# The gate's 1x1 taken for four gates at once, with common mixing tiles, and the map sets' loads moved to ScalarE's queue

## The chip, the cores and the metric

The kernel runs on one core of a Trainium2 chip. The metric is the device time of one execution, in microseconds (us). Before the change it is 9507.76 us, the median of three runs (9506.13 to 9532.57).

## What is computed

There are eight batch elements of 8 channels x 512 x 512 in float32. Layer 0 normalises the channels in groups, multiplies a few of their lowest Fourier modes and adds the result back. Layer 1, cut to what matters here (x is the normalised input):

```
grid = x
for _ in range(15):
    mapped  = 3.9 * grid * (1 - grid)
    physics = 0.7 * mapped + 0.3 * conv3x3(mapped, K, one kernel per channel)
    grid    = 0.85 * physics + 0.15 * x
cml = clip(grid, 0.0001, 0.9999)
nca = sigmoid(conv1x1(relu(conv3x3(x, Wp)), Wu))            # 8 -> 128 -> 8 channels
g   = sigmoid(conv1x1(relu(conv3x3([x, cml, nca], Wg1)), Wg2))   # 24 -> 8 -> 8, the gate
out = g * cml + (1 - g) * nca                               # then the layer's residual is added
```

## The kernel before, in words

All of it is one program, whose order is written by a planner in Python: every engine executes its instructions in the order of the source. The unit of the plan is a tick, one call of `turn` (L1044) and in it of `work` (L1013). An element takes 67 or 68 ticks, and each tick mixes work of three kinds.

- **Map steps.** The 15 steps of the map run on sets: a `Slabs` object holds 16 slabs of 32 rows, and a set has one step in every second or third tick. A tick takes two steps. `convolve` (L518) issues 48 products in 32x32 tiles on TensorE: row of tiles h takes slab group h and writes PSUM bank `ps[h // 2][..., h % 2]`, column t writes 32 partitions of it. `settle` (L531) adds the drive on VectorE (L537), squares on ScalarE (L543) and renews the slabs' edge rows by transfers within SBUF (`renew`, m<-m, L570 and L571). A set's inputs are eight loads of 256 KB, dE and dO (L495), made ahead by `Phase.fetch` (L687); the squares of the first input are L502, the drives on GpSimd L516 and L547.
- **Hidden rounds.** Up to two rounds of the 8 -> 128 convolution (`Hidden.round`, L715: 24 matmuls each, L723, relu half on ScalarE L729 and half on VectorE L731), then the 128 -> 8 product of two rounds (`Hidden.point`, L738: L742, read out by a copy on ScalarE L749 or an addition on VectorE L751, sigmoid L755, stored by L758 one tick later). Their input is cols, 512 KB for four rounds (L706).
- **Others.** The layer 0 pieces of the element after this one (`spectral`), and the gates of the element before (`Gate`, L765).

A gate makes 12 rows. Its `load` brings gin, three transfers on SyncE's queue (L778: 384, 320 and 320 KB), and mix, the same rows of x, cml and nca, three transfers of 192 KB on 96 partitions (L783). `conv` computes the 3x3 in 12 matmuls (L793), blends x and nca on VectorE (L799), subtracts on GpSimd (L798) and applies the relu on VectorE (L803). A tick later `point` does the 1x1: three products of 128 x 32 (L810), each of two passes on the chip, then the sigmoid (L814) and a product on GpSimd (L816). In the next tick `finish` adds (L821) and stores 192 KB (L828). There are 43 gates an element, 344 in all.

`Others.feed` (L902) issues the gate's loads and the spectral pieces' loads of x early in the tick, before the second step's renewals; `transfers` then calls `Phase.fetch`. All these transfers are issued by SyncE. PSUM is four pairs of banks; `near` and `far` are two of them each and change roles, so that what a tick's gate and hidden point write is next written by the second step of the following tick. SBUF's big tiles come from 20 slots, which `sets` and `shared` divide by limits set tick by tick (`SHARED, MORE, LEAST`, L66).

After the last element 80 hidden rounds and all of its 43 gates are left; they run in ticks without map steps (L1090), two rounds and one gate each, here called the last stage.

Of the kernel before, what the change touches and what calls it, by code (L numbers as in the profile page):

```python
# [35 lines left out]
F32 = mybir.dt.float32  # L36
AF = mybir.ActivationFunctionType
ALU = mybir.AluOpType
# [79 lines left out]
def conv_layers(ctx: ExitStack, tc: tile.TileContext, a, out):  # L118
# [76 lines left out]
    gband = load("w_g1", [P, 3, 32])  # L195
    gpoint = load("w_g2", [P, GR * C])
    b_p = load("b_p", [HID, 1])
# [117 lines left out]
    def layer0(e, bank):  # L315
# [89 lines left out]
        def close(g, mv):  # L405

            mean, rstd, std = yield from group_stats(mv, 1, bank)
            nc.vector.tensor_copy(means[:, 0, g : g + 1], mean)
            nc.vector.tensor_copy(means[:, 1, g : g + 1], std)
            for c in (2 * g, 2 * g + 1):  # L410
                xt = e.x[C + c]
                nc.vector.tensor_scalar(xt, xt, mean, rstd, ALU.subtract, ALU.mult)

                def store(c=c, xt=xt):
                    nc.sync.dma_start(
                        out=e.xn[1 : N + 1, c].rearrange("(p j) w -> p j w", j=4), in_=xt
                    )
                    e.done_with(C + c)
                    e.closed.append(c)

                later(1, store)
# [48 lines left out]
    class Slabs:  # L470
# [14 lines left out]

        def load(self, o, h):
            if h == 0:
                self.d[o] = sets.take([P, 4, N], "dO" if o else "dE")
            if h == 3:
                self.loaded[o] = now[0]  # L490
            at, dims = self.source(o, h)
            to = self.d[o][32 * h : 32 * h + 32]
            if len(dims) == 4:
                to = to.rearrange("p (a b) w -> p a b w", a=2)
            nc.sync.dma_start(out=to, in_=view(self.e.xn, C * N + at, dims))  # L495

# [159 lines left out]
    class Phase:  # L656
# [7 lines left out]

        def load(self):
            s, o, h = self.loads.popleft()
            s.load(o, h)

# [18 lines left out]
        def fetch(self, n):  # L687
            while n - self.at >= -AHEAD and self.loads:
                s, _, h = self.loads[0]
                begun = sum(0 in x.d or x.m is not None for x in self.sets)  # L690
                if not h and sets.room() <= begun - self.squared or len(s.e.closed) < C:
                    break
                self.load()

# [70 lines left out]
    class Gate:  # L765


        def __init__(self, e, first):
            self.e, self.first, self.r0 = e, first, min(first, N - GR)

        def load(self):

            r0, self.at = self.r0, now[0]
            self.gin = shared.take([P, 4, N], "gin")
            self.mix = shared.take([P, 4, N], "mix")
            for q, src in enumerate((self.e.xn, self.e.cml, self.e.nca)):
                at, rows = (0, 48, 88)[q], (6, 5, 5)[q]
                nc.sync.dma_start(  # L778
                    out=self.gin[at : at + rows * C],
                    in_=view(src, r0 * C * N, [[N, rows * C], [3 * C * N, 4], [1, N]]),  # L780
                )
            for q, src in enumerate((self.e.xn, self.e.cml, self.e.nca)):
                nc.sync.dma_start(  # L783
                    out=self.mix[: GR * C, q],
                    in_=view(src, (r0 + 1) * C * N, [[N, GR * C], [1, N]]),
                )

        def conv(self, ps):

            gin, (x1, d, ng) = self.gin, (self.mix[: GR * C, q] for q in range(3))  # L790
            for n, (dx, lo, hi, at) in enumerate(SHIFTS):
                for j in range(4):
                    nc.tensor.matmul(  # L793
                        ps[32 * j : 32 * j + 32, lo:hi], gband[:, dx], gin[:, j, at : at + hi - lo],
                        start=(n == 0), stop=(n == 2), tile_position=(0, 32 * j),
                    )

            nc.gpsimd.tensor_tensor(d, d, ng, ALU.subtract)  # L798
            nc.vector.scalar_tensor_tensor(  # L799
                x1, x1, self.e.back[: GR * C, 1:2], ng, ALU.mult, ALU.add  # L800
            )
            shared.drop(gin)
            nc.vector.tensor_scalar(self.mix[:, 3], ps, b_g1, 0.0, ALU.add, ALU.max)  # L803

        def point(self, ps):
            mix = self.mix
            ps = ps[: GR * C]
            for j in range(3):
                at = slice(32 * j, 32 * j + 32)
                nc.tensor.matmul(  # L810
                    ps[at], gpoint[:, at], mix[:, 3], start=True, stop=True,
                    tile_position=(0, 32 * j),
                )
            nc.scalar.activation(mix[: GR * C, 2], ps, AF.Sigmoid, bias=b_g2[: GR * C])  # L814
            d = mix[: GR * C, 1]
            nc.gpsimd.tensor_tensor(d, d, mix[: GR * C, 2], ALU.mult)  # L816

        def finish(self):

            x1, o = (self.mix[: GR * C, q] for q in range(2))  # L820
            nc.vector.scalar_tensor_tensor(  # L821
                o, o, self.e.back[: GR * C, 0:1], x1, ALU.add, ALU.add
            )
            self.store()

        def store(self):
            lo = self.first - self.r0
            nc.sync.dma_start(  # L828
                out=view(
                    out, self.e.b * C * N * N + self.first * N,  # L830
                    [[N, GR - lo], [N * N, C], [1, N]],
                ),
                in_=self.mix[C * lo : GR * C, 1],
            )
            shared.drop(self.mix)

    class Element:


        def __init__(self, b):  # L840
# [11 lines left out]
            self.hidden = Hidden(self)  # L852
            self.gates = deque(Gate(self, r) for r in range(0, N, GR))
            self.back = sm.tile([P, 2], F32, name="back", bufs=3)
            self.x, self.at, self.fetched = {}, {}, 0
# [37 lines left out]
    class Others:  # L893


        def __init__(self):
            self.before, self.after, self.limit = None, None, 2
            self.mapped, self.paused = deque(), False
            self.loaded, self.convolved, self.pointed = deque(), deque(), deque()
            self.longs = 0  # L900

        def feed(self, t):  # L902
# [5 lines left out]
            kept = max(0, after.most() - len(after.x)) if spectral else 0  # L908
            while e and e.gates and t >= GATES_FROM and not self.paused:
                if len(self.loaded) == self.limit or shared.room() - kept < 2:  # L910
                    break
                if e.rows < min(e.gates[0].r0 + GR + 1, N) or len(e.mapped) <= 2 * SETS:
                    break
                g = e.gates.popleft()
                g.load()
                self.loaded.append(g)
            if spectral:
                after.fetch()

        def busy(self):  # L920
            return self.before.gates or self.loaded or self.convolved or self.pointed

        def finish(self):
            while self.pointed:
                self.pointed.popleft().finish()

        def point(self, ps):
            if not (self.convolved and self.convolved[0].at < now[0]):
                return False
            g = self.convolved.popleft()  # L930
            g.point(ps)
            self.pointed.append(g)
            return True

# [9 lines left out]
        def gate(self, ps):  # L944
# [4 lines left out]
            g.conv(ps)  # L949
            g.at = now[0]  # L950
            self.convolved.append(g)
            return True
# [40 lines left out]
    for n in count():  # L993
# [9 lines left out]
        while (  # L1003
            len(e.closed) >= C // 2 and len(first.loads) > 8 * (SETS - 2) and sets.room()
        ):
            first.load()
    tick(end=True)
# [4 lines left out]

    def work(steps, rounds, e, after, transfers, squares=lambda: None):  # L1013

# [12 lines left out]
        next(settled, None)  # L1027
        squares()

        if rounds == 2:  # L1030
            pairs.reverse()
        elif rounds:
            near, far = far, near
        point = rounds and e.hidden.n % 2 == 0
        gate = others.gate(near[0][:, 0])
        others.spectral((far[0], far[1]) if gate else (near[0], far[0] if point else near[1]))
        if point:
            e.hidden.point(near[1][:, 0])
        if not others.point(near[0][:, 1]):
            others.spectral([near[0] if gate or point else near[1]])  # L1040
        tick()
        squares()

    def turn(at, rounds, e, after, t):  # L1044
# [4 lines left out]
        def transfers():  # L1049
            others.feed(t)  # L1050
            for p in now_phases:
                p.fetch(at)

        def squares():
# [5 lines left out]
        steps = [slots[i] for i in (at, at + 1) if 0 <= i < len(slots)]  # L1060
        work(steps, rounds, e, after and after.hidden, transfers, squares)

# [86 lines left out]
```

## Time and profile before

| | |
|---|---|
| median of three runs | 9507.76 us |
| the profiled execution | 9539.07 us, span 9537.3 us |
| mean granted TensorE clock | 0.981 |
| TensorE matmul busy | 9076.3 us, 95% of the span |
| VectorE, ScalarE, GpSimd busy | 58%, 43%, 18% |
| transfers | 1326.71 MB, 53.5% of 16 engines' time on SyncE's queue |

The profile is one execution. PE is TensorE's matmuls, PEld its weight loads, DVE VectorE, ACT ScalarE, POOL GpSimd, SP SyncE; SPq is SyncE's queue of transfers. A group's line has the source line, the engine, the operation, the tiles (out<-in), the shape and count, then busy us and mean ns, and after the second bar the idle time before it and what ended most of it. "issue" is idle time for which no wait is seen. In the timeline a line has its start, its duration and how many instructions were merged. An element's ticks are counted from 0.

### The profile page before, as it was taken

To read this page: it belongs to the slowest core of one execution; us is meant where nothing else is said; L and a number is where in the kernel's file an instruction comes from. 1 tells how busy PE (TensorE), PEld (TensorE's weight loads), DVE (VectorE), ACT (ScalarE), POOL (GpSimd) and SP (SyncE) were. 2 spreads that over 40 slices of the span, in tenths; PEclk is the share of its full clock that TensorE was granted. 3 is DMA by queue.
4 is the path that set the end of the run, shared out by engine and by line. 5 is a ranking of instruction groups with operands and counts; after the bars stand their busy time and mean duration, and the time that the engine had idled before them with its cause. 6 is when DMAs were issued, how large, how long until landed. Compare 5 with 4: busy or idle time off the path is not lost. (4 is left out here: it accounts for less than half of the span.)

```text
span 9537.3 us, 330619 instructions
## 1 busy us (share of the span) xinstructions
PE 9076.3 (95%) x148976; PEld 4075.3 (43%) x148976; DVE 5572.4 (58%) x5820; ACT 4071.8 (43%) x4285; POOL 1671.2 (18%) x1286
## 2 busy tenths in 40 slices
PE   6999999999999999999999999999999999888999
PEld 3444444444444444444444444444444444333433
DVE  5665566655665556655566555665556655454555
ACT  2444444444444444444444444444434444333432
POOL 2010111112121121211212121021211212122122
PEclk9999999999999999999999999999999999999999
DMA  4241365565555555555555546555464555565288
GB/s 146 87 127 35 90 165 137 148 142 137 157 152 142 140 130 146 160 133 136 153 135 162 146 117 172 131 158 133 120 175 131 156 142 123 138 157 139 70 203 196
DMA packets 626870, 1326.71 MB, mean 139 GB/s; under 512 B 75258, under 2 KB 80762, under 8 KB 597970
## 3 DMA queue, kind: packets, MB, share of 16 engines
q1 hardware_dynamic: 623104, 1304.42, 53.5%
q8 instruction: 1170, 19.17, 0.9%
q14 instruction: 242, 1.98, 0.1%
q10 hardware_dynamic: 2354, 1.14, 0.0%
HBM read 977.48 MB, written 270.61 MB: 131 GB/s over the span
## 5 line engine op out<-in xcount | busy, mean ns | idle before, releaser
L524 PE MATMUL pair<-m,band 32*32 32x512 f32 x103680 | 3719.4, 607 | 208.7 <-issue 124.1
L543 ACT ACTIVATE m<-m 128x1024 f32<-128x1024 f32 x2016 | 2124.5, 1055 | 2438.6 <-DVE m L537 2293.2
L723 PE MATMUL pair<-cols,w_p 32*128 32x511 f32 (+1 forms) x24576 | 2860.0, 603 | 44.8 <-ACT y L749 14.4
L524 PEld LDWEIGHTS pair<-m,band 32*32 32x32 f32 x103680 | 2005.0, 103 | 1856.4 <-issue 1052.5
L537 DVE SCALAR_TENSOR_TENSOR m<-pair,dO 128x1024 f32<-128x1024 f32 x1152 | 1356.6, 1219 | 1218.4 <-PE pair L524 973.3
L723 PEld LDWEIGHTS pair<-cols,w_p 32*128 32x128 f32 x24576 | 1310.0, 186 | 1612.4 <-issue 1158.8
L537 DVE SCALAR_TENSOR_TENSOR m<-pair,dE 128x1024 f32<-128x1024 f32 x1008 | 1187.0, 1219 | 1142.4 <-PE pair L524 902.9
L731 DVE TENSOR_SCALAR h<-pair,b_p 128x1024 f32<-128x1024 f32 x1024 | 1313.0, 1283 | 877.8 <-PE pair L723 873.4
L729 ACT ACTIVATE h<-pair,b_p 128x1024 f32<-128x1024 f32 x1024 | 1140.6, 1114 | 902.5 <-PE pair L723 902.1
L816 POOL TENSOR_TENSOR mix<-mix 96x512 f32<-96x512 f32 x344 | 438.0, 1273 | 4302.2 <-ACT mix L814 4053.3
L742 PE MATMUL pair<-h,w_u 128*32 128x512 f32 x8192 | 1059.1, 610 | 47.6 <-ACT h L729 47.5
L793 PE MATMUL pair<-gin,w_g 128*32 128x511 f32 (+1 forms) x8256 | 964.7, 600 | 4.0 <-DMA gin<-nca 2.0
L798 POOL TENSOR_TENSOR mix<-mix 96x512 f32<-96x512 f32 x344 | 442.2, 1285 | 1423.4 <-DMA mix<-nca 1134.4
L547 POOL TENSOR_SCALAR dO<-dO 128x2048 f32<-128x2048 f32 x72 | 394.5, 5491 | 1009.4 <-DVE m L537 1009.1
L742 PEld LDWEIGHTS pair<-h,w_u 128*32 128x32 f32 x8192 | 244.1, 110 | 698.1 <-issue 329.2
L755 ACT ACTIVATE y<-y,b_u 128x512 f32<-128x512 f32 x256 | 184.8, 722 | 816.9 <-DVE y L751 816.9
L793 PEld LDWEIGHTS pair<-gin,w_g 128*32 128x32 f32 x8256 | 234.5, 110 | 684.6 <-issue 463.1
L749 ACT COPY y<-pair 128x512 f32<-128x512 f32 x256 | 150.1, 586 | 634.4 <-PE pair L742 487.2
L803 DVE TENSOR_SCALAR mix<-pair,b_g 128x512 f32<-128x512 f32 x344 | 258.2, 750 | 263.0 <-PE pair L793 262.5
L810 PE MATMUL pair<-mix,w_g 128*32 128x512 f32 x2064 | 370.7, 605 | 41.9 <-DVE mix L803 38.9
L821 DVE SCALAR_TENSOR_TENSOR mix<-mix,back 96x512 f32<-96x512 f32 x344 | 313.5, 911 | 144.2 <-POOL mix L816 144.2
L516 POOL TENSOR_SCALAR dO<-dO,base 128x512 f32<-128x512 f32 x288 | 208.4, 741 | 1075.6 <-DMA dO<-xn 923.9
(87 smaller groups left out, 2632.2 us busy)
## 6 DMA issues: line engine op xcount, KB each, us to landing
gin<-xn SPq DMA_DIRECT2D x344, 384.0 KB
cols<-xn SPq DMA_DIRECT2D x256, 512.0 KB
x<-in_x SPq DMA_DIRECT2D x120, 1024.0 KB
gin<-cml SPq DMA_DIRECT2D x344, 320.0 KB
gin<-nca SPq DMA_DIRECT2D x344, 320.0 KB
dE<-xn SPq DMA_DIRECT2D x288, 256.0 KB
dO<-xn SPq DMA_DIRECT2D x288, 256.0 KB
mix<-xn SPq DMA_DIRECT2D x344, 192.0 KB
```

The source lines that it names most:

```text
L524: nc.tensor.matmul(ps[h // 2][32 * t : 32 * t + 32, h % 2], band[at, self.channel(step - 1, h, t), dx], m[at, t, dx : dx + N], start=(n == ...
L537: nc.vector.scalar_tensor_tensor(u[:, at], ps[q], FLOOR, d[:, at], ALU.max, ALU.add)
L543: nc.scalar.square(u[:, at], u[:, at])
L547: nc.gpsimd.tensor_scalar(d, d, 0.5, None, ALU.add)
L723: nc.tensor.matmul(ps[g // 2][:, g % 2, lo:hi], w_p[p, dx, i % 2], self.cols[p, i // 2, at : at + hi - lo], start=(n == 0), stop=(n == 2), ...
L729: nc.scalar.activation(h[:, :2], ps[0], AF.Relu, bias=b_p)
L731: nc.vector.tensor_scalar(h[:, 2:], ps[1], b_p, 0.0, ALU.add, ALU.max)
L742: nc.tensor.matmul(ps[32 * g : 32 * g + 32], w_u[:, r % 4], h[:, g], start=(r == self.hs[0][0]), stop=(r == self.hs[-1][0]), tile_position ...
L793: nc.tensor.matmul(ps[32 * j : 32 * j + 32, lo:hi], gband[:, dx], gin[:, j, at : at + hi - lo], start=(n == 0), stop=(n == 2), tile_positi ...
L798: nc.gpsimd.tensor_tensor(d, d, ng, ALU.subtract)
L810: nc.tensor.matmul(ps[at], gpoint[:, at], mix[:, 3], start=True, stop=True, tile_position=(0, 32 * j),)
L816: nc.gpsimd.tensor_tensor(d, d, mix[: GR * C, 2], ALU.mult)
```

## The change

The old Gate keeps only gin and its 3x3; four gates make a Quad. Their relu results go to one tile (one gate in each of four columns, the partition quarters rotated by the gate's number k), and one 1x1 of 16 products of 32x32 serves all four. Four times three rows, with 24 lines used of 32, stand on the partitions, so gpoint is [128, 32] and the mixing tiles ng, d and x1 are 128 x 4 x 512 for a quad, each loaded by four transfers of 256 KB and stored by some twelve of 64 KB. The blend is done for a quad at once on GpSimd, in halves on VectorE, one tick or more after the last of the three tiles was asked for. `feed` moves to the end of the tick, behind both steps' renewals; loads of x stay where they were (`fetch`). The map sets' loads from tick 0 on (n >= 0) are issued by ScalarE, after the relus and squares of the tick.

```diff
-            nc.sync.dma_start(out=to, in_=view(self.e.xn, C * N + at, dims))
+            queue.dma_start(out=to, in_=view(self.e.xn, C * N + at, dims))
...
-                self.load()
+                self.load(nc.scalar if n >= 0 else nc.sync)
...
     class Gate:
         def conv(self, ps):
...
+                    to = 32 * ((j + self.k) % 4)
                     nc.tensor.matmul(
-                        ps[32 * j : 32 * j + 32, lo:hi], gband[:, dx], gin[:, j, at : at + hi - lo],
-                        start=(n == 0), stop=(n == 2), tile_position=(0, 32 * j),
+                        ps[to : to + 32, lo:hi], gband[:, dx], gin[:, j, at : at + hi - lo],
+                        start=(n == 0), stop=(n == 2), tile_position=(0, to),
                     )
...
+            nc.vector.tensor_scalar(quad.relu[:, self.k], ps, b_g1, 0.0, ALU.add, ALU.max)
...
+    class Quad:
+        def load(self):
+            src = (self.e.nca, self.e.cml, self.e.xn)[len(self.mix)]
+            t = shared.take([P, 4, N], ("ng", "d", "x1")[len(self.mix)])
+            for j in range(4):
+                nc.sync.dma_start(
+                    out=t[32 * j : 32 * j + 32, : self.n],
+                    in_=view(
+                        src, (self.r0 + 1 + 3 * j) * C * N,
+                        [[N, 32], [GR * C * N, self.n], [1, N]],
+                    ),
+                )
...
+        def blend(self):
+            n, (ng, d, x1) = self.n, self.mix
+            nc.gpsimd.tensor_tensor(d[:, :n], d[:, :n], ng[:, :n], ALU.subtract)
+            for k in (0, 2):
+                k1 = min(k + 2, n)
+                nc.vector.scalar_tensor_tensor(
+                    x1[:, k:k1], x1[:, k:k1], self.e.back[:, 1:2], ng[:, k:k1], ALU.mult, ALU.add
+                )
...
+        def point(self, near):
+            n, relu, (_, d, _) = self.n, self.relu, self.mix
+            for k in (1, 3, 0, 2):
+                for j in range(4 if k < n else 0):
+                    at, to = 32 * ((j + k) % 4), 32 * j
+                    nc.tensor.matmul(
+                        near[k // 2][to : to + 32, k % 2], gpoint[at : at + 32],
+                        relu[at : at + 32, k], start=True, stop=True, tile_position=(at, to),
+                    )
+            for k in (0, 2):
+                k1 = min(k + 2, n)
+                nc.scalar.activation(
+                    relu[:, k:k1], near[k // 2][:, : k1 - k], AF.Sigmoid, bias=b_g2
+                )
+                nc.gpsimd.tensor_tensor(d[:, k:k1], d[:, k:k1], relu[:, k:k1], ALU.mult)
...
     def work(steps, rounds, e, after, transfers, fetch, feed, squares):
...
         squares()
+        fetch()
...
+        others.blend()
+        quad = others.point()
         gate = others.gate(near[0][:, 0])
...
         if point:
             e.hidden.point(near[1][:, 0])
-        if not others.point(near[0][:, 1]):
+        if quad:
+            quad.point(near)
+        else:
             others.spectral([near[0] if gate or point else near[1]])
+        feed()
         tick()
```

`Others.feed` asks for one slot a gate where it asked for two, then for the mixing tiles of a quad whose gates have all been loaded, as many as there are slots for:

```diff
+            for quad in self.quads:
+                while not quad.gates and len(quad.mix) < 3 and shared.room() > kept:
+                    quad.load()
```

`Quad.finish` adds one half of the quad (a 128 x 2 x 512 instruction on VectorE) at each of its calls in a tick and stores after the second.

## The prediction

> **What bounds the kernel now.** I read the page's busy shares and groups first, then the chain of waits near its end, then the timeline of a few ticks, and last a table of stretches.
>
> ```profile
> PE 9076.3 (95%) x148976; PEld 4075.3 (43%) x148976; DVE 5572.4 (58%) x5820; ACT 4071.8 (43%) x4285; POOL 1671.2 (18%) x1286
> ...
> L810 PE MATMUL pair<-mix,w_g 128*32 128x512 f32 x2064 | 370.7, 605 | 41.9 <-DVE mix L803 38.9
> ```
>
> PE is the bound: 95%, against 58% on DVE. The group L810 is the 1x1 that changes: 344 gates of 6 matmul instructions. Its 605 ns are ends that overlap, so the price of a gate is read from the chain, where PE hands over from group to group:
>
> ```profile
> 9200.64 5.36 PE pair L723 x48
> 9205.99 2.71 PE pair L793 x24
> 9208.70 1.72 PE pair L742 x16
> 9210.42 0.85 PE pair L810 x6
> 9211.27 5.36 PE pair L723 x48
> ```
>
> A tick of the last stage is these four, 10.63 us with no gap, 0.85 us of it the 1x1. A tick in the middle, by the timeline, is this:
>
> ```profile
> 4501.22 6.58 PE L524 MATMUL pair<-m,band 32*32 32x512 f32 x192
> ...
> 4517.40 1.03 PE L810 MATMUL pair<-mix,w_g 128*32 128x512 f32 x6
> ...
> 4517.65 0.69 DVE L751 TENSOR_TENSOR y<-y,pair 128x512 f32<-128x512 f32 x1 [0.89 <-PE pair L742]
> ...
> 4518.36 6.58 PE L524 MATMUL pair<-m,band 32*32 32x512 f32 x192
> ```
>
> The tick is 17.14 us, again packed; its first block, 192 instructions in 32x32 tiles, ends at 4507.73: 12 waves of 16 in 6.51 us, 0.543 each. Where PE does stop, the transfers are behind it. These lines are from a tick in which the loads of two gates were issued together:
>
> ```profile
> 6418.69 0.44 SPq L778 DMA_DIRECT2D gin<-xn  x1
> ...
> 6434.21 1.91 PE L524 MATMUL pair<-m,band 32*32 32x512 f32 x3 [4.34 <-issue]
> ...
> 6439.23 1.26 POOL L798 TENSOR_TENSOR mix<-mix 96x512 f32<-96x512 f32 x1 [6.32 <-DMA mix<-nca]
> ```
>
> Twelve loads, 3.28 MB, took 20.5 us from the first issue to the end of the wait for the last, 160 GB/s, and meanwhile PE stood 4.3 us inside a block with no wait of its own. The last stage is closest to the limit of the transfers; four ticks, with the columns span, PE, PEld, DVE, ACT, POOL, clock, DMA share, GB/s:
>
> ```profile
> 9185.00:9227.50 42.50, 42.50 (x380) 15.23 (x376) 23.77 (x23) 14.02 (x17) 9.95 (x8) 1.00 0.86 213
> ```
>
> PE is busy 42.5 of 42.5 us, and the transfers already fill 86%.
>
> **The change, part by part.** Where ticks and orders of the changed program are named, they are from the listings of the two built programs.
>
> 1. *The old 1x1 goes.* 344 x 0.853 us (17.14 less 16.29, a tick without it: 6.51 + 5.36 + 2.60 + 1.83) = -293 us, all on PE's path.
>
> 2. *88 waves come*, each 16 products in two passes: 2 x 0.543 = 1.1 us at the least. But the last four products write the bank that the NCA's 1x1 (L742) has just filled, and must wait for its reading. The timeline has this: without L810 the next block would have begun at 4518.36 - 0.85 = 4517.51, while L751 reads until 4518.34. The wave's last quarter starts at about 4518.42, then half a wave's rest and the second pass take 0.9: 1.8 us. 88 x 1.8 = +158. Bounds: 0.9 (no wait) and 3.4 (the four products of a bank one after another, 4 x 2 x 0.43, L742's 1.72 us being four sets of four), +80 and +300.
>
> The Trainium skill, TensorEngine Tiling (Array Packing), Restrictions and Gotchas, says that different row tiles cannot access the same PSUM bank at once. L524 gives each row of tiles a bank of its own, the new wave puts four rows of tiles in one bank, in four quarters of the partitions, and no row here shows that; by the page, read strictly, the 3.4 would hold and the sum would be 142 us higher.
>
> I take the row of L524, as the nearest: also 32x32, also 16 tiles at once.
>
> 3. *Mixing tiles.* They grow from 576 KB a gate to 3 x 1024 KB a quad, 9.70 MB instead of 8.91 in four ticks of the last stage, and come in bursts. In 37 of the 88 quads all three are issued in one tick, with a gate's 1 MB: 4.1 MB. The blend follows in the next tick: two DVE instructions, which wait for the last of the three tiles, and behind them on DVE stand the gate's relu, the addition to y and the next settles. So here is a new wait.
>  - Last stage: the burst starts about 5.4 us into its tick (the 512 KB of cols ahead of it in SP's queue wait for the second round). The table gives 211 / 0.87 = 241 GB/s at full share, the two-gate row 160: 4.1 MB take 17 to 26 us, with the 0.77 MB of other transfers 20 to 31. DVE reaches the blend 17.8 us after the burst's tick began (a tick of 9.8 with the wave's 1.8, then two rounds of 5.4 and 0.8 of relu), so it stands 8 to 19 us. After it come 2 x 1.22 (L537's row, same size) + 0.75 + 0.69 = 3.9 us, and PE needs the banks at 24.1 (11.6 + 9.8, and one round of 2.7). PE loses 5 to 16 us. I take 8, nearer to the fast end, since SP runs ahead where nothing holds it: 10 quads, +80. Bounds 0 and +160.
>  - First half of the last element: ticks of 13 to 14 us, six such quads, 2 to 10 us by the same working; 6 each, +36 (0 to 60).
>  - First halves of elements 1 to 6: ticks of 18.3 us, two each, 0 to 5 us; 2 each, +24 (0 to 60).
>
> 4. *The map sets' loads on ScalarE.* What they cost the engine that issues them is shown on SP:
>
> ```profile
> 1642.76 2.12 SPq L495 DMA_DIRECT2D dE<-xn  x4
> 1644.92 2.92 SPq L495 DMA_DIRECT2D dO<-xn  x4
> 1648.93 4.10 SPq L495 DMA_DIRECT2D dE<-xn  x4
> ```
>
> Twelve loads hold their queue 10.3 us, for the program lets only a few transfers be in flight and each issue waits for an earlier landing. ACT works 8 to 12 us of such a 16.6 us tick. Runs of 4 fit beside that; 8 nearly. Runs of 12 or 16 come once in each of elements 0 to 6: the squares and relus of the next tick then start 2 to 7 us late, and PE waits for the relus before L742. Five runs of 12 at 3 us, two of 16 at 7: +30. Bounds 0 and +120 (every run of 8 or more pays its whole landing). On the other side the renewals of m and the gates' loads no longer queue behind these loads, and feed now stands behind both renewals of a tick: the page has 37.3 us of PE and 73.8 of PEld waiting for m<-m; I credit -30 (0 to -100).
>
> The skill's DMA: Bandwidth & Descriptors, Issuing engines are not separate DMA queues, holds that another issuing engine saves only issue time. By it the credit is 0 and the sum 30 higher. The trace has no second queue at work to weigh this.
>
> 5. *Bursts and PE's own stops.* The 4.3 us stop above recurs where transfers fill a tick's first block; L524's idle time put to issue is 124.1 us in all. More ticks issue over 4.5 MB than before: +40 (0 to +124).
>
> 6. *Taken at nothing.* DVE does less (two 128x1024 instructions for four 96x512). POOL's work is the same per element: after the sigmoids' 1.1 us two products of 2 x 1.27 us end 6.2 us after the wave, and DVE asks for the first 5.7 us into the next tick (L821's place): hidden, else 0.5 us a quad. SP issues 12 stores of 64 KB for four of 192 KB, at 0.83 us for L828 some 10 us in one tick; behind them stand that tick's second renewals, which are due two ticks later.
>
> Sum: -293 + 158 + 140 + 30 - 30 + 40 = +45 us. The profiled execution took 9539.1 us (span 9537.3), so 9584; the median of the runs shown is 31 us under the profiled one, so **9553 us** is forecast.
>
> **The rivals.**
> - *Faster: the tiles land in time.* If the three tiles land before DVE reaches the blend, part 3 falls from 140 to 20, and with quieter transfers part 5 to 0: -115, 9393 us. It turns on the burst's landing: under about 20 us after its first issue in the last stage it costs PE under 5 us. For it: 241 GB/s is the rate at full share, and SP may issue early. Against: 160 in the two-gate row.
> - *Slower: the wave is no wave.* Products in a bank run one by one, 3.4 us a quad: +142, 9695 us. So the change wouldn't do what it says. For it: no such wave in the trace; against: L524.
> - *Slower: ACT is held.* The loads wait out whole landings and relus start late each time: +90 on the sum, 9643 us. For it: 4.10 us for the last four above; against: ACT is idle half of the tick.
>
> **How the numbers follow.** My forecast has 0.42: with its own spread of 60 us, 0.06 of that is faster by over 0.3%, 0.12 within, 0.24 slower (0.3%, 29 us, is about what a measurement of this kernel can tell from no change). Tiles in time: 0.30, all faster. ACT held: 0.18, of it 0.02 within. No wave: 0.10, slower. Together faster 0.36, same 0.14, slower 0.50. The range leaves out one tenth on each side: 9375, just below the first rival, to 9695, the second. Both signs hold much: the forecast's own range is 9490 to 9615.
>
> **What would show it.** The new 1x1 at 1.8 us from L742 to the next block, two passes of 16; DVE's blend waiting for x1 in the last stage, and ticks there of over 10.6 us on average; ACT idle in the middle of runs of loads with PE waiting for h before L742; L524 waiting less for m<-m. I am wrong if the blend doesn't wait in the last stage, or if L524 loses or gains far more than 40 us.

## The result and the profile after

The changed kernel takes 10510.78 us (median of 4 runs, 10492.92 to 10526.2), the kernel before 9520.17 beside it: the ratio is 1.104, 95% interval 1.1011 to 1.1068. That is 990 us slower. The forecast of 9553 us, made as 45 us over the 9507.76 known then, is 33 over this median of the kernel before, and its range ended at 9695. The profiled execution has a span of 10506.0 us.

The page, first the busy times, then groups (busy, mean ns of one | idle time before them and what ended most of it):

```profile
PE 9169.1 (87%) x149664; PEld 4091.7 (39%) x149664; DVE 5544.4 (53%) x5484; ACT 4021.0 (38%) x4117; POOL 1607.1 (15%) x862
...
L525 PE MATMUL pair<-m,band 32*32 32x512 f32 x103680 | 3881.3, 623 | 747.5 <-DVE relu L796 209.9
...
L724 PE MATMUL pair<-cols,w_p 32*128 32x511 f32 (+1 forms) x24576 | 2936.1, 607 | 167.7 <-ACT y L750 115.6
...
L750 ACT COPY y<-pair 128x512 f32<-128x512 f32 x256 | 150.0, 586 | 1095.2 <-DMA nca<-y 495.5
L831 DVE SCALAR_TENSOR_TENSOR x<-x,back,ng 128x1024 f32<-128x1024 f32 (+1 forms) x176 | 231.7, 1357 | 593.0 <-DMA x<-xn 421.9
```

The same two groups of PE in the page before, and the wait of ACT's copy for the store of y (us, times, longest):

```profile
L524 PE MATMUL pair<-m,band 32*32 32x512 f32 x103680 | 3719.4, 607 | 208.7 <-issue 124.1
...
L723 PE MATMUL pair<-cols,w_p 32*128 32x511 f32 (+1 forms) x24576 | 2860.0, 603 | 44.8 <-ACT y L749 14.4
```
```profile
ACT y L749 <- DMA nca<-y: 36.9, 6, 15.5
```

PE falls from 95% to 87%. Its idle time ahead of the convolutions (L525, before: L524) is 747.5 us where it was 208.7, ahead of the hidden rounds 167.7 where it was 44.8. Two waits stand behind most of it: DVE's blend waits 422 us for x1, as feared, and ACT's copy L750 of y waits 495 us for the *store* of the y before it (36.9 us before), which no step of the forecast names.

The wave itself does what it says. From the timeline, one quad in a middle tick (the answer to the row of L810 before):

```profile
4681.23 1.90 PE L743 MATMUL pair<-h,w_u 128*32 128x512 f32 x16
4683.05 1.51 PE L844 MATMUL pair<-relu,w_g 32*32 32x512 f32 x20
4684.13 0.61 PE L525 MATMUL pair<-m,band 32*32 32x512 f32 x1
4684.33 0.67 PE L844 MATMUL pair<-relu,w_g 32*32 32x512 f32 x12
4684.58 6.86 PE L525 MATMUL pair<-m,band 32*32 32x512 f32 x191
```

From the wave's start to the block behind it 1.53 us go by for four gates, where four of the old 1x1 took 4 x 0.853 = 3.4. The tick before shows where it is lost; the timeline's columns are start, length, engine or queue, and instruction (wait in brackets):

```profile
4628.09 2.00 SPq L815 DMA_DIRECT2D ng<-nca  x4
4630.25 12.19 SPq L815 DMA_DIRECT2D d<-cml  x4
...
4643.42 0.34 SPq L759 DMA_DIRECT2D nca<-y  x1
...
4651.20 1.73 SPq L815 DMA_DIRECT2D x<-xn  x4
...
4651.72 0.59 ACT L750 COPY y<-pair 128x512 f32<-128x512 f32 x1 [18.88 <-DMA nca<-y]
...
4652.35 4.70 PE L525 MATMUL pair<-m,band 32*32 32x512 f32 x96 [12.96 <-ACT y L750]
```

SP needs 12.19 us to issue four loads of d, for each stands until an earlier transfer has landed (next fence); the store of y is planned behind them, goes out at 4643.42 and has landed only when ACT goes on, 8 us later. The bank with the next y is not read until then, and PE stands 12.96 us. SP's waits for the mixing tiles' issues, in us, times, longest:

```profile
SPq L815 <- DMA gin<-nca: 176.6, 63, 4.4
...
SPq L815 <- DMA gin<-cml: 145.6, 63, 4.9
SPq L815 <- DMA ng<-nca: 111.1, 139, 2.2
```

In the last stage four ticks took 42.5 us at 213 GB/s; now they take 55.4, columns as in the prediction's table, and in the third of them both waits end within 0.4 us of each other:

```profile
10117.22:10172.62 55.40, 45.71 (x389) 15.66 (x385) 21.32 (x18) 13.55 (x14) 9.16 (x3) 0.91 0.78 173
```
```profile
10150.67 2.48 DVE L831 SCALAR_TENSOR_TENSOR x<-x,back,ng 128x1024 f32<-128x1024 f32 x2 [12.17 <-DMA x<-xn]
10151.02 0.59 ACT L750 COPY y<-pair 128x512 f32<-128x512 f32 x1 [15.45 <-DMA nca<-y]
...
10151.66 6.82 PE L724 MATMUL pair<-cols,w_p 32*128 32x512 f32 x24 [9.26 <-ACT y L750]
```

Here 24 instructions of L724 last 6.82 us, against 2.7 elsewhere: the stop is followed by half clock (last section), and in their midst the weight loads wait 1.71 us more for DVE's relu L796.

Where the time went, as sums of tick lengths (from a tick's first product to the next tick's first, in the last stage to its last product) of the two traces:

| stage | before | after |
|---|---|---|
| elements 1 to 6, ticks 0 to 7 | 847 | 889 |
| ticks 8 to 15 | 886 | 1075 |
| ticks 16 to 23 | 828 | 949 |
| ticks 24 to 31 | 852 | 1003 |
| ticks 32 to 47 | 1605 | 1685 |
| ticks 48 to 55 | 818 | 945 |
| ticks from 56 | 1114 | 1067 |
| element 0 / element 7 | 985 / 940 | 1013 / 1058 |
| last stage | 474 | 626 |

Some gates also run at other times now: ticks 8 to 23 hold 18 more of their 3x3 products than before (2.6 us each), ticks 32 to 47 eight more, and the ticks from 56 none where 24 stood. These last ticks are the only ones that got shorter, by less than those 24 took. Single ticks stand out: over elements 1 to 6, tick 9 takes 34.7 us (before 18.9), tick 26 35.2 (15.6), tick 48 28.2 (17.4).

### The profile page after: what moved, and what is told of

Its sections match the earlier page's. It is cut to its first block, busy times and chain, and to the rows that moved or that the text cites. A ratio compares the mean times of both kernels' runs of the same rounds, so it can differ in the third digit from the quotient of the medians.

```text
span 10506.0 us, 330319 instructions
## 1 busy us (share of the span) xinstructions
PE 9169.1 (87%) x149664; PEld 4091.7 (39%) x149664; DVE 5544.4 (53%) x5484; ACT 4021.0 (38%) x4117; POOL 1607.1 (15%) x862
## 5 line engine op out<-in xcount | busy, mean ns | idle before, releaser
L525 PE MATMUL pair<-m,band 32*32 32x512 f32 x103680 | 3881.3, 623 | 747.5 <-DVE relu L796 209.9
L724 PE MATMUL pair<-cols,w_p 32*128 32x511 f32 (+1 forms) x24576 | 2936.1, 607 | 167.7 <-ACT y L750 115.6
L525 PEld LDWEIGHTS pair<-m,band 32*32 32x32 f32 x103680 | 2046.6, 105 | 2438.3 <-issue 1045.1
L724 PEld LDWEIGHTS pair<-cols,w_p 32*128 32x128 f32 x24576 | 1339.7, 188 | 1797.0 <-issue 1199.4
L743 PE MATMUL pair<-h,w_u 128*32 128x512 f32 x8192 | 1078.0, 618 | 62.4 <-ACT h L730 57.5
L789 PE MATMUL pair<-gin,w_g 128*32 128x511 f32 (+1 forms) x8256 | 972.6, 604 | 48.4 <-DMA gin<-nca 28.3
L828 POOL TENSOR_TENSOR d<-d,ng 128x2048 f32<-128x2048 f32 (+1 forms) x88 | 393.1, 4467 | 3374.5 <-DMA m<-m 1209.2
L853 POOL TENSOR_TENSOR d<-d,relu 128x1024 f32<-128x1024 f32 (+1 forms) x176 | 417.3, 2394 | 2433.4 <-issue 1328.9
L750 ACT COPY y<-pair 128x512 f32<-128x512 f32 x256 | 150.0, 586 | 1095.2 <-DMA nca<-y 495.5
L831 DVE SCALAR_TENSOR_TENSOR x<-x,back,ng 128x1024 f32<-128x1024 f32 (+1 forms) x176 | 231.7, 1357 | 593.0 <-DMA x<-xn 421.9
L743 PEld LDWEIGHTS pair<-h,w_u 128*32 128x32 f32 x8192 | 244.3, 111 | 742.3 <-issue 393.4
L789 PEld LDWEIGHTS pair<-gin,w_g 128*32 128x32 f32 x8256 | 238.1, 110 | 735.4 <-issue 541.9
L796 DVE TENSOR_SCALAR relu<-pair,b_g 128x512 f32<-128x512 f32 x344 | 257.6, 749 | 457.6 <-PE pair L789 391.7
L860 DVE SCALAR_TENSOR_TENSOR d<-d,back,x 128x1024 f32<-128x1024 f32 (+1 forms) x176 | 272.6, 1549 | 60.6 <-POOL d L853 55.7
```

What stands on the lines that cost most here:

```text
L525: nc.tensor.matmul(ps[h // 2][32 * t : 32 * t + 32, h % 2], band[at, self.channel(step - 1, h, t), dx], m[at, t, dx : dx + N], start=(n == ...
L724: nc.tensor.matmul(ps[g // 2][:, g % 2, lo:hi], w_p[p, dx, i % 2], self.cols[p, i // 2, at : at + hi - lo], start=(n == 0), stop=(n == 2), ...
L743: nc.tensor.matmul(ps[32 * g : 32 * g + 32], w_u[:, r % 4], h[:, g], start=(r == self.hs[0][0]), stop=(r == self.hs[-1][0]), tile_position ...
L789: nc.tensor.matmul(ps[to : to + 32, lo:hi], gband[:, dx], gin[:, j, at : at + hi - lo], start=(n == 0), stop=(n == 2), tile_position=(0, to),)
L828: nc.gpsimd.tensor_tensor(d[:, :n], d[:, :n], ng[:, :n], ALU.subtract)
L853: nc.gpsimd.tensor_tensor(d[:, k:k1], d[:, k:k1], relu[:, k:k1], ALU.mult)
```

## The experiments

Four theories of the 990 us. **S**: SP's order, the store of y behind the feed's loads. **D**: DVE standing at the blend. **A**: the map sets' loads and ACT. **V**: the volume of the bursts, which stops whoever waits for it last, so that a cured wait comes back under another name. All ratios are to the kernel before, run beside.

### One cause at a time, in the changed kernel

*stores_first*: the loads are planned where they were and issued behind the stores.

```diff
         feed()
         tick()
+        for issue in issues:
+            issue()
```

> The loads of a tick's feed are planned where the changed kernel plans them, but issued on SP behind the stores that fall due at the tick's end (nca<-y first) instead of ahead of them; nothing else moves. Three theories of the +990 us. S, SP's order: the store of y stands behind up to 15 loads, y has one buffer, so ACT's copy L750 of the next y waits for the landing (495 us in 45 waits in the changed kernel, 37 in 6 before) and PE waits for ACT (L525 180 us, L724 116 us, and part of the 200 us of waits for h L730). D, DVE at the blend: L831 waits 422 us for x1 and 144 us more under another name, PE behind it 210 us for relu L796 and 141 us for y L752. V, volume: the burst of 4 MB needs its time, and whoever waits for it last stops PE whatever the order. S expects 250 to 400 us less than 10511 (10110 to 10260) and the wait of L750 for the store below 100 us; D expects 0 to 80 less; V expects within 100 of 10511, with the waits under other names.

Measured: 10413.18 us, ratio 1.0936 (1.0917 to 1.0954), 98 less. The wait of L750 for the store falls from 495 us to 20, as S has it, yet of its 250 to 400 us not 100 came. The waits in this run, of PE, ACT and DVE (its L801 and L840 are L796 and L831 of the changed kernel):

```profile
PE pair L525 <- DVE relu L801: 224.0, 29, 29.2
PE pair L525 <- DVE y L752: 157.1, 28, 16.6
PE pair L724 <- DVE relu L801: 126.3, 9, 15.8
```
```profile
ACT y L750 <- DMA nca<-y: 20.0, 4, 14.7
```
```profile
DVE x L840 <- DMA x<-xn: 540.0, 45, 32.0
```

PE's stop ahead of L724 has changed its name, from ACT's y to DVE's relu, and the blend's wait has grown from 422 to 540 us.

*blend_late*:

```diff
                 if len(quad.mix) == 3 and quad.loaded < now[0] and not quad.blended:
+                    quad.blended = quad.due = True
...
+                if quad.due:
+                    quad.due = False
                     quad.blend()
...
             e.hidden.point(near[1][:, 0])
+        others.blends()
         if quad:
             quad.point(near)
```

> The blend (POOL's L828 and DVE's two L831) is issued in the same tick, but behind the gate's relu and the addition to y instead of ahead of them; the sizes, the loads and SP's order are as in the changed kernel. D expects 250 to 400 us less than 10511 (10110 to 10260): the 210 + 141 us of PE's waits for relu L796 and y L752 go, and the 6.5 us of the next tick's first block cover part of what is left. S expects 0 to 80 less, since ACT still waits for the store of y; V expects within 100, the wait moving to the settles of the next tick.

Measured: 10390.09, ratio 1.0906 (1.089 to 1.0922), 121 less: D is as real as S and as far from the whole. PE's waits behind relu L796 at L525 fall from 210 us to 22, and its wait for the renewals m<-m grows from 49 to 170.

*loads_sp*:

```diff
-                self.load(nc.scalar if n >= 0 else nc.sync)
+                self.load(nc.sync)
```

> Only the queue of the map sets' loads goes back from ACT to SP, at the place in the tick where the changed kernel has them. If ACT's holding is a main cause (PE waits 97 us for h L730 at L429 and 57 at L743, ACT 225 us for landings of dE and dO): 100 to 200 us less than 10511. If SP's order is (S), ACT's issues are a relief for SP, and the loads put in front of the stores again cost 0 to 100 us more.

Measured: 10524.5, ratio 1.1049 (1.1033 to 1.1066): no gain. The queue alone is not it: ACT no longer stands at the issues, but its squares L503 now wait 340 us for dE where they waited 138.

*all_three*: the three edits above.

> The three edits together: loads behind the stores, the blend behind relu and y, the map sets' loads on SP. If S and D each hold and are separate, 500 to 750 us less than 10511 (9760 to 10010), still above before by the stalls of the bursts; V expects less than 200 us less. If it were below 9520 the wave itself would be worth its 150 us, and only the order of the rest would be at fault.

Measured: 10270.13, ratio 1.0782 (1.0766 to 1.0798), 241 less, little over the sum of the parts (205), and under half of the 500 to 750 that S and D promised together, if over the under 200 of V alone. What PE waits for now:

```profile
PE pair L525 <- DMA m<-m: 174.8, 22, 19.7
...
PE pair L743 <- DVE h L732: 110.3, 22, 17.5
PE pair L794 <- DMA gin<-nca: 105.4, 27, 16.8
```

The renewals m<-m (48.6 us in the changed kernel) and gin (28.3) are the next in the same burst. That is how V has it; the bytes themselves are tried next.

### The volume

*three_quarters* and *half*: 

```diff
-                    out=t[32 * j : 32 * j + 32, : self.n],
+                    out=t[32 * j : 32 * j + 32, : min(3, self.n)],
...
-                        [[N, 32], [GR * C * N, self.n], [1, N]],
+                        [[N, 32], [GR * C * N, min(3, self.n)], [1, N]],
```

(2 for 3 in *half*; the blend reads the loaded rows for the others.)

> The loads of a quad's three mixing tiles bring the rows of three of its four gates; the blend takes the last gate's from the third, so its sizes stay (one more instruction on DVE and two on POOL), and the output's rows of every fourth gate are wrong: this leaves out a quarter of 264 MB. What is left, 2304 KB a quad, is what four gates of the kernel before loaded. The runs so far gave 97 us for SP's order, 121 for the blend's place, 0 for the queue, 240 together, out of 990: so V is the favourite, in two forms. V-sum (the sum of bytes): most of the 890 us that are left go, below 9800. V-burst (all three tiles in one or two ticks, 4 to 6 MB where a tick before had 2 to 3): the bursts are 0.77 MB shorter, 3.3 us at 230 GB/s, in 88 quads up to 290 us: 10200 to 10350. D and S alone, which are about order: within 60 of 10511.

Measured: 10269.6, ratio 1.0796 (1.0779 to 1.0812), 241 less.

> The same with the rows of two of a quad's four gates loaded, and the other two computed from these: DVE's instructions and sizes are those of the changed kernel, POOL's are two of half the size; half of the output's rows are wrong, and half of 264 MB is left out, 65 MB less than the kernel before loaded for the same purpose. V-sum: at or below before's 9520. V-burst: 1.54 MB a burst less, 6.7 us, up to 590 us: 9900 to 10150. S and D: within 100 of 10511.

Measured: 10018.53, ratio 1.0529 (1.0511 to 1.0546), 492 less. Both lie where V-burst put them, and with as many bytes as the kernel before moved (*three_quarters*: 1331 MB in the whole trace, 1327 before) the kernel is still 8% slower, the two moves in the schedule included: not the sum of bytes, but their coming together. By the traces' totals 62.9 MB are left out in *three_quarters* and 132.1 in *half*, so each MB costs 241 / 62.9 = 3.8 and 492 / 132.1 = 3.7 us, most of its transfer at the 223 to 239 GB/s of a burst (last section; 4.4 to 4.7 us for 1024 KB).

*no_mixing_loads* loads no mixing tile; GpSimd fills each with a constant (1.77 us a tile):

```diff
-            for j in range(4):
-                nc.sync.dma_start(
...
+            nc.gpsimd.memset(t[:, : self.n], 0.5)
```

> The changed kernel without the loads of the mixing tiles: each tile is filled with a constant by GpSimd instead, so the blend, the wave and the rest keep their instructions and the output is wrong. It leaves out 264 MB. The runs with three quarters and with half of them fell by 242 and 493 us, 3.7 us for each MB; a straight line on gives 9520 to 9560 here. Then the bytes of the bursts, and not the blend's order, are what the mixing tiles cost, and what is left above the 9350 that the wave's gain of 150 alone would give is the late feed and the map sets' loads. If the standing of DVE and SP has other causes, it stays above 9700.

Measured: 9741.84, ratio 1.0223 (1.0204 to 1.0242). The loads of the mixing tiles cost 769 us, 8.7 a quad. The second half of the bytes (138.5 MB) was worth only 277 of them, 2.0 us for each MB, so the price of a MB falls once the bursts are short, and the straight line failed: 222 us are left that no mixing tile can explain. The 769 us are against no such loads at all. What the old ones cost in the kernel before was not run; there PE stood 461 us in all (9537.3 - 9076.3), and no wait of PE names a load of mix.

### The other two parts, in the kernel before

*before_act* has the map sets' loads on ACT at the new place, *before_place* on SP at the new place:

```diff
         squares()
+        fetch()
...
             others.feed(t)
+
+        def fetch():
             for p in now_phases:
                 p.fetch(at)
```

> The kernel before, with the one part of the change that moves the map sets' loads: issued by ACT, behind the tick's relus and squares. My forecast put it at +30 for ACT and -30 for earlier renewals, 0 in sum; the queue alone, put back in the changed kernel, gave 14 us more. If ACT's holding costs what ACT's 24 us stop in tick 26 of the changed kernel suggests (six elements, 10 to 20 us each): 60 to 120 us above 9520.

Measured: 9707.02, ratio 1.0205 (1.019 to 1.022), 196 more.

> The kernel before, with the map sets' loads at the changed kernel's place in the tick (behind the hidden rounds and the squares), but still issued by SP. The same with ACT's queue took 9707, 196 us above before. If ACT's standing is the cause, 9500 to 9560 here; if the place is (the loads start 5 to 11 us later and land in the next tick's way), 9650 to 9750.

Measured: 9647.78, ratio 1.0125 (1.0105 to 1.0146), 127 more. So two thirds are the place, one third ACT's standing. At the new place the squares of the next tick wait on ACT for loads that started later; the kernel before, then *before_place*:

```profile
ACT m L502 <- DMA dE<-xn: 135.9, 30, 11.3
```
```profile
ACT m L502 <- DMA dE<-xn: 269.8, 45, 19.4
```

The cost sits where the loads come in runs: ticks 24 to 31 of elements 1 to 6 take 852 us before, 947 with ACT and 903 with SP.

*before_late* issues the gates' loads at the end of the tick, *before_late_sf* the same behind the stores:

```diff
         def transfers():
-            others.feed(t)
+            others.fetch(t)
...
+        feed()
         tick()
```

> The kernel before, with the gates' loads (3 of gin, 3 of mixing rows for each gate, every gate for itself) issued at the end of the tick instead of behind its second settle. S: these six issues now stand in front of the store of y as in the changed kernel, so the wait of ACT's copy of y for that store grows from 37 us, and the time by 50 to 150 us. V: no burst is added, so within 30 of 9520.

Measured: 9729.12, ratio 1.0223 (1.0203 to 1.0243), 218 more; over S's 150, and V's 30 is refuted for this part. But the wait by which S works did not grow (36.9 us before). PE's stops without a seen wait did, from 124.1 us, and its wait for gin, from 2.0:

```profile
ACT y L749 <- DMA nca<-y: 39.0, 4, 16.1
```
```profile
PE pair L524 <- issue: 195.4, 108, 4.1
...
PE pair L793 <- DMA gin<-nca: 35.8, 12, 10.1
```

> The kernel before, with the gates' loads planned at the end of the tick as in the run that took 9729, but issued behind the stores that fall due there instead of ahead of them. S: the store of y is no longer held up, so 9520 to 9600. If the late start of the loads is the cause whatever stands behind them (they meet the next tick's renewals and PE's stops without a wait grew from 124 to 195 us), 9690 to 9760.

Measured: 9652.51, ratio 1.0128 (1.0112 to 1.0145): 132 more than the kernel before. So 86 of the 218 are SP's order, though not by the store of y, and 132 the late start: the stops without a seen wait are back at 120.7 us, and PE waits 101 us for gin. Each of the two moves in the schedule, without a wave or a quad, costs 2%.

### Together

*early_loads*: queue and place of the map sets' loads undone in the changed kernel.

```diff
-                self.load(nc.scalar if n >= 0 else nc.sync)
+                self.load(nc.sync)
...
             others.fetch(t)
-
-        def fetch():
             for p in now_phases:
                 p.fetch(at)
+
+        def fetch():
+            pass
```

> The changed kernel with the map sets' loads on SP and at their old place, behind the second settle: the second half of the change undone whole, and nothing else. In the kernel before that half cost 196 us with ACT's queue and 127 with SP's; the queue alone, put back here, gave nothing (10525). If the parts add up, 100 to 200 us less than 10511; if the bursts cover what this half costs, within 50.

Measured: 10406.22, ratio 1.0927 (1.0906 to 1.0948), 105 less.

*all_four*: this, *stores_first* and *blend_late*.

> The changed kernel with four edits: the feed's loads behind the stores due at the tick's end, the blend behind relu and y, the map sets' loads on SP again, and at their old place behind the second settle. The first three gave 10270 together. If the place is worth here what the two together cost in the kernel before, 10050 to 10120; if the bursts rule, 10220 to 10290.

Measured: 10136.33, ratio 1.064 (1.0623 to 1.0656): another 134 on *all_three*. The bursts remain.

*wave_alone*: *no_mixing_loads*, *early_loads* and *stores_first*.

> The changed kernel with its three other costs taken away: no loads of mixing tiles (each tile filled with a constant by GpSimd, so the output is wrong and 264 MB are left out), the map sets' loads on SP at their old place, the feed's loads of gin behind the stores due at the tick's end. What is left of the change is the wave with its relus, blend and products. My forecast for the wave against the old 1x1 was -293 + 158 = -135 us. If that holds, and the late start of gin's loads costs up to the 132 us it cost in the kernel before, 9380 to 9520; if the wave itself were slower than forecast (3.4 us each), above 9620.

Measured: 9650.41, ratio 1.0129 (1.0104 to 1.0154), above the first range and within the one given to a slow wave. The wave is not slow, though: here too its 2752 instructions are 170 us busy of PE against 371 of the old 1x1. One stop stands out, in tick 26 of elements 1 to 6; from this run's timeline:

```profile
4009.47 2.00 ACT L503 ACTIVATE m<-dE,mhalf 128x2048 f32<-128x2048 f32 x1 [14.45 <-DMA dE<-xn]
...
4018.46 2.00 ACT L503 ACTIVATE m<-dE,mhalf 128x2048 f32<-128x2048 f32 x1 [6.88 <-DMA dE<-xn]
...
4024.35 2.10 PE L429 MATMUL pair<-e,ty 8*128 8x512 f32 x4 [20.12 <-ACT h L730]
```

By the plan, a quad drops its tiles at once, two map sets get slots in one tick, 16 loads are planned in it (before: 4, 12, 4 over three ticks), and their squares come in the next tick, on ACT ahead of the hidden relus.

*wave_alone_sq* moves the squares a tick away from their loads, *wave_alone_lim* allows 8 loads of a phase in a tick (without the edit to the squares):

```diff
-                if not self.ready(self.squared, 0, n + 2):
+                s = self.sets[self.squared]
+                due = self.at + self.squared <= n + 3
+                if not (0 in s.loaded and (s.loaded[0] < now[0] - 1 or due)):
```

> The run that left the wave alone (no mixing loads, so a wrong output and 264 MB less; loads on SP at their old place; feed behind the stores) took 9650, where the wave's terms alone give 9385. Its trace shows tick 26 at 37 us in each element, 16 in the kernel before: the plan, with a quad's tiles dropped at once, frees slots for two map sets in tick 25, issues their 16 loads in it, and ACT's squares L503 of tick 26 stand up to 14.5 and 6.9 us for dE, ahead of the hidden relus L730, for which PE stands 20 us. Here the squares come one tick later after their loads, nothing else moves. If that is what is left: 20 us in seven elements, 9480 to 9560. If the stop only moves to the next wait for the same bytes: within 40 of 9650.

Measured: 9549.25, ratio 1.0022 (1.0012 to 1.0031), 101 less: over elements 1 to 6 tick 26 falls from 36.7 to 17.6 us, and tick 27 takes 8 of these back.

```diff
-            while n - self.at >= -AHEAD and self.loads:
+            for _ in range(8 if n >= 0 else 99):
+                if n - self.at < -AHEAD or not self.loads:
+                    break
```

> The same kernel without mixing loads, with at most 8 of a phase's map loads in a tick instead of up to 16; the squares as in the changed kernel. If the bunch of 4 MB in tick 25 is the cause, 9480 to 9580; if what counts is that a square comes one tick after its own loads, however few, 9600 to 9680.

Measured: 9614.32, ratio 1.0093 (1.0066 to 1.012), 36 less. It is the tick between load and square that counts, more than the bunch.

*all_five*: *all_four* with the squares a tick later.

> The changed kernel, complete, with the four edits that gave 10136 together and the squares one tick later after their loads. If the stop of tick 26 is separate from the mixing tiles' bursts, 9990 to 10050; if the bursts of the following ticks take its place, 10080 to 10150. Above before's 9520 in any case, by what the bursts cost.

Measured: 10066.11, ratio 1.0564 (1.0546 to 1.0582), 70 less, between the two ranges. It is the best version with every load in it, and still 5.6% slower than before. No run beats the kernel before.

## Why the prediction was wrong

1. *The old 1x1, -293*, and 2. *88 waves, +158*: right as far as the runs show. The two waves read take 1.53 us (fence above) and, in the last stage, 1.93, where 1.8 was taken; over the 87 waves behind which PE goes on, the median is 1.54 us and the sum 154 us, waits inside included. The way there was partly another: in the last stage twelve of a wave's sixteen products, not four, wait for the reading of L742's bank (their weight loads stand 0.73 us for DVE's y L752), and then start together. The rival that it is no wave (3.4 us) is refuted, and with it the strict reading of the Trainium skill's TensorEngine Tiling (Array Packing), Restrictions and Gotchas, that different row tiles cannot access one bank at once: four rows of tiles in one bank did not take turns (last section). The -135 of both terms was never run by itself: *wave_alone_sq*, at 9549, still has the late start of gin, for which PE waits 66 us and which cost the kernel before 132. With the kernel before beside it, 9530 - 135 + 132 = 9527 comes within 22 us, but that is a sum and no measurement, and this run also lacks the loads of the mixing tiles.

3. *Mixing tiles, +140*: the failed step. Without their loads the changed kernel takes 769 us less. (The 140 were meant over the old loads, whose own cost is not known.) The forecast saw the burst, its 4.1 MB and its 17 to 31 us, but let one group of instructions pay, DVE's blend, in 28 of the 88 quads. It put the other 60 at nothing without a reason, and in the last stage it counted on SP running ahead "where nothing holds it". SP is held: each issue stands for an earlier landing (12.19 us for four loads), so a burst also holds everything that is planned behind it on SP. The forecast followed the loaded tile to who reads it, and did not list who else stands in that queue: the store of y, on whose landing ACT's one buffer of y depends; the renewals; the next gin. Nor is it the order alone: the stores ahead of the loads brought 98 us, the blend behind relu and y 121. Ticks 40 to 55 of elements 1 to 6, priced at nothing, lost 197 us net.

4. *Map sets' loads, +30 and -30*: 105 us in the changed kernel, 196 in the kernel before. The renewals' credit had the wrong sign, by little: PE's wait behind m<-m for the convolutions grew, from 37.3 us to 45.2 in *before_act* and 51.5 in *before_place*. The runs of 12 and 16 were seen and priced by the time ACT takes to issue them, but not that the squares of the next tick wait on ACT for their landing, which no queue cures (a tick between load and square brought 70 us in *all_five* and 101 in *wave_alone_sq*, both with the loads on SP). The rule of the Trainium skill's DMA: Bandwidth & Descriptors, Issuing engines are not separate DMA queues, that another issuing engine saves only issue time, fits *loads_sp* (nothing) and says nothing of the 69 us (196 less 127) by which ACT's queue was dearer than SP's at one place.

5. *Bursts and PE's own stops, +40*: they didn't grow in the changed kernel. L525's idle time put to issue is 115.5 us, 124.1 before. (In *before_late* they did, to 195.4.)

6. *SP at nothing*: wrong, by a move that this part leaves out. The feed at the tick's end costs 218 us in the kernel before, 86 for what it stands in front of, and 132 for its late start. The forecast used this move only as part of the renewals' credit.

Left out altogether: the clock. The mean granted clock fell from 0.981 to 0.941. The same instructions in the groups of L525, L724, L743 and L789 are busy 8868 us, 8603 before, 265 more; a part of that is stops inside blocks, how much was not separated.

The rival "tiles land in time" fell with the first fence; "ACT is held" had the direction of part 4 and a tenth of the miss.

The parts, all but the -135 measured singly, -135 + 132 to 218 + 105 + 70 to 101 + 769, make 941 to 1058 us against 990. They overlap, as the curing of one wait at a time showed, so this is no proof that nothing is missing. Open stays whether the same bytes spread over the ticks would cost nothing: feed at its old place, or one mixing tile a tick, was not tried.

## What to carry to other kernels

When loads are bundled, price the burst for everything that is planned behind it on the same queue, and follow the stores above all: a late store holds a single-buffered tile, that tile holds an engine, and that engine holds a PSUM bank. If curing the wait that the profile names gives a quarter of its microseconds, take bytes out instead of waits: the slope per MB helps to tell order from volume. And a change in three parts deserves three separate runs on the old kernel: two of these parts cost more there (196 and 218 us) than the third was to gain (135).

## What the runs showed of the hardware

*A stop of PE is paid twice.* In tick 26 of an element of the changed kernel, by stretches (the last three columns: granted clock, DMA share, GB/s):

```profile
4231.00:4240.00 9.00, 9.00 (x217) 4.91 (x216) 6.73 (x8) 0.00 (x0) 0.00 (x0) 1.00 0.85 225
4240.00:4250.00 10.00, 3.30 (x32) 1.41 (x24) 2.87 (x3) 0.00 (x0) 2.71 (x4) 0.78 0.93 239
4250.00:4260.00 10.00, 0.00 (x0) 0.00 (x0) 0.00 (x0) 6.36 (x7) 0.00 (x0) 0.50 0.97 223
4260.00:4270.00 10.00, 7.54 (x44) 1.59 (x60) 2.51 (x3) 5.06 (x7) 2.71 (x4) 0.53 0.41 97
```

PE stops at 4243.3, the clock falls to 0.5, and PE's first 7.5 us of work after the stop run at about half speed (four instructions of L429 take 2.10 us, 1.03 ahead of the stop). In the trace the granted clock changes in steps of 3.413 us. Counting the windows of this trace that were at full clock: where PE was busy for under 0.3 of a window the next one was at half clock, 93 times of 93; for 0.3 to 0.5, 28 of 43; for 0.5 to 0.9, 23 of 251. Once at half, it stayed there until a window was busy for more than 0.8 of its length. By the two mean clocks, with the rest at full clock, the span holds about 362 us of half clock before (2 x 0.019 x 9537) and 1240 after (2 x 0.059 x 10506). The Trainium skill's TensorE: Matmul & The Clock Gate, Part 1, has the same 3.4 us and the same half rate, after an idle window; here windows that were partly busy sufficed.

*Four rows of 32x32 tiles write one bank at once*, in four quarters of the partitions. In the wave at 4683.05 us the four products of the first bank, each from another row of tiles, start within 20 ns of one another and their second passes 0.45 us later; the twelve of the other three banks then start within 81 ns, and the block behind the wave 1.53 us after its start. One after another, the four products of each bank would have taken the forecast's 3.4 us.
